# Two groups of row-tile products turned round and one transpose moved up, in the last stage of a four-block fused kernel

## The chip, the core and the metric

The kernel runs on one core of a Trainium2 chip. A core has five engines that run beside each other, each with its own queue of instructions: TensorE (PE, matrix products; its weight loads are shown apart as PEld), VectorE (DVE), ScalarE (ACT), GpSimd (POOL) and SyncE (SP), which here issues DMAs. Products are written to PSUM, in banks of 128 x 512 float32; the other operands lie in SBUF. The metric is the device time of one execution in microseconds (us).

## The reference, cut to what matters

The reference chains four blocks over `x` of 16 batches x 256 tokens x 256 features, each added to `x` through a gate: a resampler's cross attention, a top-2 mixture of experts, a masked cross attention, and at last a gated linear attention with a dense and a routed part. The change lies in the last one. Cut to what is touched:

```python
x = layernorm(x)
g1 = log_sigmoid(x @ Wg1a @ Wg1b + bg1) / 16     # decay of the dense part
g2 = log_sigmoid(x @ Wg2a @ Wg2b + bg2) / 16     # decay of the routed part
g  = x @ Wga @ Wgb                               # gate of the output
q1, k1, v = x @ Wq, x @ Wk, x @ Wv
...
o = chunked_attention(q1, k1, v, g1) + routed_attention(q2, k2, v, g2)
o = o * rsqrt(mean(o * o) + eps) * norm_w * (g * sigmoid(g))
out = x + tanh(gate) * (o @ Wo)
```

All products that share `x` and have narrow outputs (`Wqa`, `Wka`, `Wga`, `Wg1a`, `We`, `Wg2a`) are taken together, as one product with a matrix `la` of 256 columns; its result is called `low`.

## The kernel before, in words

Everything is float32, and a product shows in the profile as two records, its two passes. The last stage is the function `stage3_fast` (from L1619). It handles the 16 batches one after the other, and each batch in four slots, one for each pair of heads. A slot has a number `p` from 0 to 63; its batch is `p // 4`, and `p % 4` says which slot of the batch it is. The loop over `p` writes out the order of the work by hand: in each slot the main steps stand at fixed places, and small tables (`start`, `middle`, `rest`, `late`, `behind_mask`, `by_rows`, `logs`, L2036 to L2045) hang further steps on the slots. An entry `(f, d)` in list 0 to 3 calls `f` for batch `p // 4 + d` in that slot. Each engine runs its instructions in the order in which these calls issue them. Most instructions of VectorE, ScalarE and GpSimd show the line L50, that of a helper that records them, so they are told apart by the tiles that they write; products show L1637 and PE transposes L1640.

The main steps of a slot, in order: `masked(p - 1, 1)` (VectorE masks the second score block of the slot before, out of a PSUM tile of two banks called `sc`, of which there is one), `keys_queries(p + 1)` (products `kq`), the table `middle`, the table `rest`, `decays(p + 1)` (products `gq` and `gz`, then exponentials `ee` on ScalarE), the table `late`, `products(p, 0)` (products `sc<-f`), `masked(p, 0)` (VectorE, `at<-sc,amask`), the table `behind_mask`, `factors(p + 1)` (VectorE writes `f` from `kq` and `ee`, which frees the bank of `kq`), the table `by_rows`, `values` of the slot before (products `o`), `second(p + 1)` and `factors_second(p + 1)` (VectorE writes `q` from `gq` and `ee`, POOL writes `k`), the table `logs`, and `products(p, 1)` (products `sc<-q,k`). In the fourth slot `pairs` (products `both`, then VectorE's `em` and `am`) stands ahead of all.

Three steps matter here.

`turn_ahead(b)` (L1685) turns the normalised rows `xn` of the batch after next into `xnT`, with features on the partitions. VectorE transposes 32 x 32 squares in one instruction (`turned<-xn`), and 16 DMAs issued by SyncE (L1693) carry the squares to their places in `xnT`. There are two `xnT` buffers, for even and odd batches. It is called in the third slot, from the table `logs`, for batches 2 to 15. The first reader of the new `xnT` is `lows(b)` (L1695), two slots on, in the first slot of the next batch: eight passes `low<-xnT,la`, right behind `keys_queries`.

`lows(b)` also starts two DMAs that put copies of rows of `low` on other partitions: `lowd` (L1706, rows 0 to 63 copied to 64 to 127) and `low2` (L1708, rows 64 to 127 of the second 128 tokens copied to 0 to 63). With a copy on other partitions, two products with few rows lie in different row tiles of PE, which can run at the same time.

`all_gates(b)` (L1758), in the second slot, takes four products of 17 rows each: two that read `low` itself (row tiles from 64 and 96, tokens 0 to 127, written to two banks called `z`), and two that read `low2` (row tiles from 0 and 32, tokens 128 to 255, written to the tile `sc`). ScalarE reads the first `z` bank, then the two banks of `sc`; the second `z` bank is read later, by `gates_end`.

`outgates(b)` (L1811), in the first slot of its own batch, takes four products of 64 rows for the gate of the output: in turn one that reads `low` (rows 0 to 63) and one that reads `lowd` (rows 64 to 127), written to two banks called `zg`. The `lowd` that it reads was carried in the first slot of the batch before.

The order of each group, and the place of `turn_ahead`, as they stand before:

```python
                for i in range(2):
                    for n, (lo, hi) in enumerate(((0, 17), (32, 49))):
                        x, w = (low2[lo:hi, :], lbg2[lo:hi, :]) if i else (low[b][64 + lo:64 + hi, 1, tokens(0)],
                                                                         lbg[64 + lo:64 + hi, :])
                        matmul(two[:, n, :] if i else one[n], x, w, start=True, stop=True)
...
            behind_mask = {0: [(route_logits, 1)]}
...
                    2: [(gate_logs, 1, 1), (turn_ahead, 2), (normed_out, -1, 0), (normed_out, -1, 1)]}
```

Of the kernel before, what the change touches and what calls it, by code (L numbers as in the profile page):

```python
# [73 lines left out]
def layers(ctx: ExitStack, tc: tile.TileContext, t, out, check):  # L74
# [797 lines left out]
    def w3_load(name, shape, src=None):  # L872
        x = c3(name, shape)
        src = t[src or name]
        weights.append((x, src if len(src.shape) == len(shape) else src.rearrange("(k p) f -> p k f", p=P)))
        return x
# [3 lines left out]
    lbg = w3_load("lbg", [P, 512])  # L880
# [738 lines left out]
    def stage3_fast(early_bank):  # L1619

        with ExitStack() as sx:
# [3 lines left out]
            def of(b):  # L1625

                return w1 if b % 2 else w0

            def bank(name):
                return pss.tile([P, 512], F32, tag="ps", name=name) if pss else early_bank(name)  # L1630

            def tokens(i):
                return slice(i * P, (i + 1) * P)


            def matmul(*a, **k):
                tc.keep_in_program_order(nc.tensor.matmul(*a, **k))  # L1637
# [7 lines left out]
            lbg2 = w1.tile([P, 512], F32, tag="lbg2", name="lbg2")  # L1645
# [7 lines left out]
            xn, xnT, low, lg, hT, em, am, lowd = {}, {}, {}, {}, {}, {}, {}, {}  # L1653
# [104 lines left out]
            def all_gates(b):  # L1758

                lg[b] = of(b).tile([P, 2, 2, 512], F32, tag="lg", name="lg")  # L1760
                two = psa.tile([P, 2, 512], F32, tag="sc", name="sc")
                one = [bank("z"), bank("z")]
                for i in range(2):
                    for n, (lo, hi) in enumerate(((0, 17), (32, 49))):
                        x, w = (low2[lo:hi, :], lbg2[lo:hi, :]) if i else (low[b][64 + lo:64 + hi, 1, tokens(0)],
                                                                         lbg[64 + lo:64 + hi, :])
                        matmul(two[:, n, :] if i else one[n], x, w, start=True, stop=True)
                act3.activation(lg[b][:, 0, 0, :], one[0], AF.Exp, scale=-1.0)
                act3.activation(lg[b][:, 1], two, AF.Exp, scale=-1.0)
                z_[b, "z"] = one[1]  # L1770
# [40 lines left out]
            def outgates(b):  # L1811

                gw[b] = w2.tile([P, 4, S], F32, tag="gw", name="gw")
                two = [bank("zg"), bank("zg")]
                for i in range(2):
                    for h, (w, x) in enumerate(((lbg[0:64], low[b][0:64, 1, :]), (lbg2[64:], lowd[b][64:]))):
                        m = 2 * i + h
                        matmul(two[h][:, i * S:(i + 1) * S], w[:, m * P:(m + 1) * P], x, start=True, stop=True)
                for h, ps in enumerate(two):
                    e, zs = (w2.tile([P, 512], F32, tag=n, name=n) for n in ("eg", "zs"))  # L1820
                    act3.activation(e, ps, AF.Exp, scale=-1.0)
                    dve3.tensor_copy(zs, ps)
                    z_[b, h] = zs, e
# [205 lines left out]
            def warm():  # L2029

                ps = bank("warm")
                for _ in range(2):
                    matmul(ps, ones, v[B - 1][:, 0, :], start=True, stop=True)


            start = {3: [(pairs, 1)]}  # L2036
            middle = {0: [(lows, 1)], 1: [(all_gates, 1)], 2: [(turn_hot, 1)], 3: [(scaled_first, 0)]}

            rest = {0: [(bias, 2)], 2: [(turned_hot, 1), (norm_ahead, 2)], 3: [(steepest, 1, 0), (steepest, 1, 1)]}
            late = {1: [(norms, -1)], 2: [(vals, 1)], 3: [(project, -1)]}  # L2040
            behind_mask = {0: [(route_logits, 1)]}
            by_rows = {0: [(outgates, 0)], 1: [(gates_end, 1)]}
            logs = {0: [(route_sums, 1), (outgates_end, 0, 0)],
                    1: [(route, 1), (stats, 2), (outgates_end, 0, 1), (gate_logs, 1, 0)],
                    2: [(gate_logs, 1, 1), (turn_ahead, 2), (normed_out, -1, 0), (normed_out, -1, 1)]}  # L2045

            def run(steps, p):
                for f, d, *a in steps.get(p % 4, ()):
# [75 lines left out]
            b, p = B - 1, last - 1  # L2124
# [39 lines left out]
    if fast:  # L2164
        with tc.tile_pool(name="ctx_side", bufs=1) as keep, tc.tile_pool(name="f12w2", bufs=2) as keep2:
            prep = Prepare(keep, keep2, shared_bank)
            stage1_fast(keep, prep, shared_bank)
            s1.close()
            last_stage = stage3_fast(shared_bank)
            next(last_stage)  # L2170
            stage2_fast(prep, shared_bank, last_stage)
            next(last_stage)
        s_banks.close()
        for _ in last_stage:
            pass
    else:
        stage1()
        s1.close()
        stage2()
        s12.close()  # L2180
        stage3()
# [69 lines left out]
```

## Time and profile before

| What | Value |
|---|---|
| timed runs, median of three | 1838.59 us (1833.2 to 1842.05) |
| the profiled execution's own time | 1836.71 us |
| span of its records | 1834.8 us |
| mean granted TensorE clock | 0.995 |
| last stage's slots | from about 1237 to 1820 us |
| one batch of the last stage (start of its second slot's first `z` product to the next batch's) | 36.69 to 38.96 us |
| SyncE's issues of the 16 DMAs of one `turn_ahead` | 10.34 us for batch 8 |
| PE's wait for `xnT`, the longest one | 2.6 us |

The span is the time from the first record to the last; the execution's own time holds 1.9 us more around it. In the views, a row of the timeline has the start, the length, the engine, the line, the operation, the tiles written and read (`out<-in`), the form and the number of instructions that were merged into it; in brackets stands the idle time ahead of it and what ended that. In a view of waits a line has who waited, for whom, the total in us, how many times, and the longest. In the view of windows the columns are the stretch, its length, the busy time of each engine with the number of instructions, the granted TensorE clock as a share of full speed, and the DMA engines' share and rate.

### The profile page before, as it was taken

The page shows a single profiled execution, that of the slowest core. Times are in us where ns is not written, and L with a number is a line of the kernel's source. Part 1 is how long each engine was busy: PE and PEld are TensorE (multiplying, and loading weights), DVE is VectorE, ACT ScalarE, POOL GpSimd, SP SyncE. Part 2 cuts the span into 40 slices and gives each one's busy share as a digit, 9 for nine tenths or more (in the row PEclk, how much of TensorE's full clock was granted, in tenths as well). Part 3 has the DMA queues.
Part 4 walks back from the last instruction along what each step waited for, and adds up shares of the span by engine and source line. Part 5 has one row for each costly group of instructions (what it writes and reads, how often), then busy time and mean ns, then how long its engine had stood idle before and what let it go on. Part 6 is the DMA issues. An engine that isn't in the chain of part 4 may idle for free.

```text
span 1834.8 us, 35411 instructions
## 1 busy us (share of the span) xinstructions
PE 1802.7 (98%) x13930; PEld 1246.4 (68%) x13930; DVE 1138.6 (62%) x2695; ACT 832.4 (45%) x1727; POOL 1014.3 (55%) x1001
## 2 busy tenths in 40 slices
PE   8999999999999999999999999999999999999997
PEld 5666666666666666666777866656777777777775
DVE  3345656666656666666475388866666666666664
ACT  4433345343453334434343488744543454445432
POOL 3654766567666576656743766314454445444533
PEclk9999999999999999999999999999999999999999
DMA  9800010000010000000067933100111111111110
GB/s 298 235 1 22 16 35 13 28 17 20 27 35 10 29 20 10 28 24 17 13 221 246 251 56 48 21 3 11 38 28 36 29 37 28 34 31 32 33 31 26
DMA packets 110361, 98.05 MB, mean 53 GB/s; under 512 B 43835, under 2 KB 97763, under 8 KB 109673
## 3 DMA queue, kind: packets, MB, share of 16 engines
q1 hardware_dynamic: 97897, 78.91, 14.5%
q0 software_dynamic: 12288, 16.79, 4.5%
q8 instruction: 112, 1.84, 0.4%
q14 instruction: 64, 0.52, 0.1%
HBM read 52.03 MB, written 38.41 MB: 49 GB/s over the span
## 4 chain that ended last, share of the span: by engine, by line
PE 84%; POOL 7%; DVE 3%; issue 2%; ACT 2%; SPq 1%; DMA 1%; POOLq 0%; ACTq 0%; DVEq 0%
PE o L50 11%; PE qk L50 11%; PE v L50 9%; PE sc L50 8%; PE proj L50 7%; PE kq L1637 6%; PE sc L1637 6%; PE gq L1637 4%; POOL es L50 4%; PE ex L50 3%; PE v L1637 3%; PE o L1637 3%; PE proj L1637 2%; PE low L1637 2%; PE gz L1637 2%
## 5 line engine op out<-in xcount | busy, mean ns | idle before, releaser
L50 POOL TENSOR_SCALAR rs<-mv 128x2 f32<-128x2 f32 (+2 forms) x85 | 16.2, 190 | 404.4 <-DVE mv L50 402.6
L50 DVE RECIPROCAL rd<-o 128x256 f32<-128x256 f32 x64 | 112.3, 1754 | 155.0 <-PE o L50 155.0
L50 ACT ACTIVATE e<-sc 128x1024 f32<-128x1024 f32 (+1 forms) x192 | 181.5, 1015 | 18.5 <-PE sc L50 18.5
L50 POOL TENSOR_TENSOR at<-at,at 128x768 f32<-128x768 f32 x63 | 114.1, 1812 | 134.3 <-DVE at L50 134.3
L50 PE MATMUL sc<-qk 64*128 64x256 f32 (+1 forms) x1536 | 183.1, 384 | 0.5 <-DVE qk L50 0.5
L50 PE MATMUL o<-e,v 128*32 128x256 f32 (+1 forms) x3072 | 177.9, 379 | 0.0
L50 PEld LDWEIGHTS sc<-qk 64*128 64x128 f32 (+1 forms) x1536 | 132.0, 172 | 55.1 <-issue 26.8
L50 POOL TENSOR_TENSOR esum<-esum,es 128x512 f32<-128x512 f32 x128 | 163.2, 1275 | 10.0
L50 PE MATMUL qk<-kvT,wkv 128*128 128x333 f32 x512 | 164.3, 443 | 0.0
L50 POOL TENSOR_TENSOR es<-e 128x1024 f32<-128x1024 f32 x64 | 151.3, 2364 | 12.0 <-ACT e L50 9.0
L50 ACT ACTIVATE qk<-qk 128x256 f32<-128x256 f32 x128 | 48.7, 381 | 232.2 <-PE qk L50 232.2
L50 POOL TENSOR_TENSOR es<-es,e 77x1024 f32<-77x1024 f32 x64 | 150.3, 2349 | 5.0
L50 PEld LDWEIGHTS o<-e,v 128*32 128x32 f32 (+1 forms) x3072 | 99.8, 110 | 66.4
L50 DVE TENSOR_TENSOR at<-sc,amask 128x768 f32<-128x768 f32 x64 | 61.2, 957 | 133.7 <-PE sc L1637 78.2
L50 PE MATMUL qk<-kvT,wq 128*128 128x256 f32 x512 | 134.6, 385 | 0.0
L50 DVE COPY qk<-qk 128x333 f32<-128x333 f32 x128 | 64.6, 505 | 94.8 <-ACT qk L50 93.4
L50 POOL DMA_INDIRECT x<-rows_out,pos x64 | 100.9, 1577 | 35.6 <-issue 16.5
L50 PEld LDWEIGHTS qk<-kvT,wq 128*128 128x128 f32 x512 | 94.3, 189 | 35.1 <-issue 9.6
L50 PEld LDWEIGHTS qk<-kvT,wkv 128*128 128x128 f32 x512 | 97.2, 190 | 30.0
L50 PE MATMUL proj<-wo0h,oT 128*128 128x256 f32 x512 | 113.7, 380 | 0.3 <-DVE oT L50 0.3
L50 PE MATMUL v<-wkv,kvT 128*128 128x512 f32 x256 | 113.1, 595 | 0.0
L50 PEld LDWEIGHTS proj<-wo0h,oT 128*128 128x128 f32 x512 | 96.0, 190 | 13.9 <-issue 0.8
(267 smaller groups left out, 3920.8 us busy)
## 6 DMA issues: line engine op xcount, KB each, us to landing
rows<-zero SPq DMA_DIRECT2D x16, 640.0 KB
xin<-rows SPq DMA_DIRECT2D x16, 640.0 KB
r<-rms SPq DMA_DIRECT2D x30, 256.0 KB
rows_out<-y SPq DMA_DIRECT2D x16, 384.0 KB
v<-vctx SPq DMA_DIRECT2D x15, 308.0 KB
x<-in_x_dram SPq DMA_DIRECT2D x16, 256.0 KB
rows_out<-y SPq DMA_DIRECT2D x16, 256.0 KB
out_dram<-x SPq DMA_DIRECT2D x15, 256.0 KB
```

Source lines behind the costliest of these rows:

```text
L50: x = getattr(self.engine, name)(*a, **k)
L1637: tc.keep_in_program_order(nc.tensor.matmul(*a, **k))
```

## The change

Three edits. In `all_gates` the two products that read `low2` now stand ahead of the two that read `low`. In `outgates` each pair now begins with the product that reads `lowd`; which bank each product writes stays as it was. And `turn_ahead` moves from the table `logs` to the table `behind_mask`, still in the third slot: its transpose now stands on VectorE right behind `masked(p, 0)` and ahead of `f` and `q` of the next slot. The 16 DMAs keep their place in SyncE's order, and the instructions of ScalarE and POOL keep theirs. No instruction is added or removed but for semaphore waits.

```diff
@@ all_gates
-                for i in range(2):
+                for i in (1, 0):
                     for n, (lo, hi) in enumerate(((0, 17), (32, 49))):
@@ outgates
                 for i in range(2):
-                    for h, (w, x) in enumerate(((lbg[0:64], low[b][0:64, 1, :]), (lbg2[64:], lowd[b][64:]))):
+                    for h, w, x in ((1, lbg2[64:], lowd[b][64:]), (0, lbg[0:64], low[b][0:64, 1, :])):
                         m = 2 * i + h
@@ tables of stage3_fast
-            behind_mask = {0: [(route_logits, 1)]}
+            behind_mask = {0: [(route_logits, 1)], 2: [(turn_ahead, 2)]}
...
-                    2: [(gate_logs, 1, 1), (turn_ahead, 2), (normed_out, -1, 0), (normed_out, -1, 1)]}
+                    2: [(gate_logs, 1, 1), (normed_out, -1, 0), (normed_out, -1, 1)]}
```

## The prediction

> **What bounds the kernel now.** I read the page first: busy times, then the chain that ended last.
>
> ```profile
> PE 1802.7 (98%) x13930; PEld 1246.4 (68%) x13930; DVE 1138.6 (62%) x2695; ACT 832.4 (45%) x1727; POOL 1014.3 (55%) x1001
> ...
> PE 84%; POOL 7%; DVE 3%; issue 2%; ACT 2%; SPq 1%; DMA 1%; POOLq 0%; ACTq 0%; DVEq 0%
> ```
>
> TensorE (PE) is busy nearly all the time and owns 84% of the chain. So an edit pays only where it takes a wait of PE away, and costs only where it adds one. The change lies in the last stage, from about 1237 to 1820 us. The view of waits over that stretch, for PE alone, has one large entry:
>
> ```profile
> PE low L1637 <- DMA xnT<-turned: 3.7, 4, 2.6
> ```
>
> These are the products of `lows`, the first readers of the rows that `turn_ahead` carries by 16 DMAs. The view counts only gaps over 150 ns, so I went to the timeline of PE. `lows` stands behind the four query passes of `keys_queries`, and follows them at once when its rows are there:
>
> ```profile
> 1267.82 1.03 PE L1637 MATMUL kq<-xnT,wq 128*128 128x256 f32 x4
> 1271.46 3.60 PE L1637 MATMUL low<-xnT,la 128*128 128x256 f32 x8 [2.61 <-DMA xnT<-turned]
> ...
> 1604.44 1.03 PE L1637 MATMUL kq<-xnT,wq 128*128 128x256 f32 x4
> 1605.31 1.89 PE L1637 MATMUL low<-xnT,la 128*128 128x256 f32 x8
> ...
> 1752.31 1.03 PE L1637 MATMUL kq<-xnT,wq 128*128 128x256 f32 x4
> 1753.74 1.99 PE L1637 MATMUL low<-xnT,la 128*128 128x256 f32 x8 [0.40 <-DMA xnT<-turned]
> ```
>
> The pair at 1604 is clean: `low` starts 0.87 us behind the start of the query row. At 1752 it is 1.43, so 0.56 us is lost; at 1267 it is 3.64, so 2.77 us is lost. The same subtraction for batches 3 to 15 gives 0, 0.38, 0.23, 0, 0.30, 0.05, 0.34, 0.01, 0, 0.04, 0.60, 0.22, 0.56: 2.7 us.
>
> The change by its two halves follows.
>
> **The transpose, moved up.** The timelines of DVE and SP around one `turn_ahead` (batch 8):
>
> ```profile
> 1480.26 0.96 DVE L50 TENSOR_TENSOR at<-sc,amask 128x768 f32<-128x768 f32 x1 [3.79 <-POOL k L50]
> 1481.13 0.68 DVE L50 TENSOR_TENSOR f<-kq,ee 128x512 f32<-128x512 f32 x1
> 1481.73 0.41 DVE L50 TENSOR_TENSOR q<-gq,ee 128x256 f32<-128x256 f32 x1
> 1482.07 0.71 DVE L50 STREAM_TRANSPOSE turned<-xn 128x512 f32<-128x512 f32 x1
> 1483.11 0.42 DVE L50 SCALAR_TENSOR_TENSOR em<-both,dmask 128x256 f32<-128x256 f32 x1 [0.32 <-PE both L1637]
> ...
> 1482.85 10.34 SPq L1693 DMA_DIRECT2D xnT<-turned  x16
> ```
>
> SP's 16 issues start 0.07 us behind the transpose's end and take 10.34 us. The rows land some 1.3 to 1.8 us later (`low` starts that far behind the last issue wherever it waited). From the transpose's start that is 12.4 to 13.1 us, while PE reaches `lows` 12.54 us after it (1482.07 to 1494.61). The two are even, which is why some batches wait and others don't.
>
> Now the transpose goes behind `at`, ahead of `f` and `q`: it starts at 1481.13, 0.94 us earlier. Its input `xn` was ready (ScalarE's two rows ended at 1477.65). SP's queue keeps its order and is empty there (the row before, `r<-rms`, ended at 1474.40), so all 16 DMAs move up by 0.94. That is more than every loss in batches 3 to 15 (at most 0.60), so those waits go. The `low` row also shortens from about 1.97 to 1.89, since the first weight load no longer waits. As a cross-check I took the start of the first `z` product in each batch's second slot: the periods are 38.96, then 36.72 to 37.38, the shortest 36.69 with no wait in it. From 1281.82 to 1762.49 there are 13 periods, 480.67 us; 13 x 36.69 is 476.97. Gain **3.70 us**, the row shortening included.
>
> What is delayed: `f` and `q` by one transpose, 0.62 us as DVE starts its next (0.71 less the overlap that the rows show). `f` then ends at 1482.43; it frees the bank that PE's next `kq` product takes at 1483.00, so 0.5 us of cover. `q` ends at 1482.77, ahead of `em`, which waits for PE until 1483.11 anyway. So DVE is level again before anyone asks: cost 0. If that cover were gone it would be at most 0.62 x 14 = 8.7 us.
>
> Batch 2 keeps a wait, because its first slots have no `proj` products to fill the time: its gap goes from 2.61 to 1.67 us, gain **0.94**. There is more in that batch. Its `low` row lasts 3.60 us and not 1.97, and the windows view says why:
>
> ```profile
> 1271.40:1275.20 3.80, 3.74 (x11) 3.12 (x12) 0.10 (x1) 0.00 (x0) 0.00 (x0) 0.56 0.02 4
> ```
>
> The granted clock, third from the end, is 0.56 behind the gap; 3.60 - 1.97 = 1.63 us is the price. Whether a 1.67 us gap still brings it, this trace can't say outright. Stretches of 3.41 us in which PE was busy for 0.90 us (1267.94 to 1271.36) and 2.74 us (1223.57 to 1226.98) were followed by half clock; stretches with 2.25 (from 1052.91) and 2.51 (from 1206.50) weren't. The new stretch would have 1.74 or more, depending on where the gap falls. The bounds are 0 and 1.63; I take **1.63**, the nearest row being 2.25, but not by much. [...]
>
> **The products, turned round.** `all_gates` (15 times) and `outgates` (16 times). Batch 7's `all_gates` on PE, DVE and ACT:
>
> ```profile
> 1466.57 0.70 PE L1637 MATMUL z<-lbg,low 17*128 17x512 f32 x2
> 1467.09 0.70 PE L1637 MATMUL sc<-lbg,low 17*128 17x512 f32 x2
> 1467.10 0.59 PE L1637 MATMUL z<-lbg,low 17*128 17x512 f32 x2
> ...
> 1468.15 0.71 PE L1637 MATMUL gq<-dmask,lg 128*128 128x128 f32 x4
> ...
> 1469.80 0.81 PE L1637 MATMUL sc<-f 64*128 64x256 f32 x6
> ...
> 1465.66 1.37 DVE L50 SCALAR_TENSOR_TENSOR at<-sc,kden,am 128x256 f32<-128x256 f32 x4
> ...
> 1467.72 0.60 ACT L50 ACTIVATE lg<-z 128x512 f32<-128x512 f32 x1 [1.47 <-PE z L1637]
> 1468.26 1.02 ACT L50 ACTIVATE lg<-sc 128x1024 f32<-128x1024 f32 x1
> ```
>
> The `sc` pair is the one with the DMA's rows, but its DMA was issued 5 us before and no view shows a wait for it. What holds `sc` is its PSUM bank, which DVE's masking frees at 1467.03. `z`, in other row tiles, runs in that time, and its second pass runs beside `sc`'s first. With `sc` first, PE waits until 1467.09 with both pairs; then all four run side by side. `sc` ended the group before and ends it after (`z` is some 0.013 us behind it): +0.013 x 15 = **0.2 us**. No gain is possible here, since `sc` starts no earlier.
>
> But ACT gets `z` later. Its order is `z` first, then `sc`, and it waits for `z` already. `z`'s second pass moves from 1467.10 to 1467.64, so `lg<-z` starts at 1468.26, `lg<-sc` at 1468.80, and that ends at 1469.82 where it ended at 1469.29. PE's `sc<-f` takes the bank that `lg<-sc` frees, 0.055 us after it: 1469.87, and not 1469.80. The first group shows this wait in pure form: `lg<-sc` at 1245.09 for 1.02 us and `sc<-f` at 1246.17. So +0.075 x 14 = **1.05 us**; in the first group, whose masking ends 0.54 us later still, **0.54**. ACT's next rows slide by 0.54 us and have room: it is idle for 0.47 us at 1472.2 and 1.8 at 1474.7.
>
> `outgates` alternates between the lower 64 rows (`low`) and the upper 64 (`lowd`); its DMA is a whole batch old. The group ends with the upper tile in both orders, which is busy with `sc<-f` until 1461.60 in both. ACT reads it only at 1463.2. Cost 0, bounded by one start's shift of 0.13 x 16 = 2.1 us.
>
> **Sum.** -3.70 - 0.94 - 1.63 + 0.2 + 1.05 + 0.54 = -4.5 us. The profiled execution took 1836.71 us (span 1834.8 and 1.9 around it), so 1832.2 for one like it. The median of the three timed runs, 1838.59, lies 1.88 above it: **1834.1 us**.
>
> **Rivals.** (a) Half clock stays in batch 2: 1834.1 + 1.63 = 1835.7. For it, the stretch with 2.74 us busy; against it, the two with 2.25 and 2.51. (b) The moved transpose starts no DMA earlier, the change not doing what it says: the waits view of SP names `PE both` for 11 of these issues. Then the products' price alone is left, 1838.59 + 1.8 = 1840.4. Against it: SP issued at 1482.85 while `both` ran until 1483.07. (c) Slower: the four products of `all_gates` don't run side by side after the DVE wait, and `z` comes a pass behind `sc`: 0.53 x 15 = 8.0, so 1842.1. It decides from 0.3 us per group on (4.5 / 15). Against it: `sc` at 1467.09 and `z` at 1467.10 ran together. (d) Row tiles start strictly in program order, so the lower tile in `outgates` waits for the upper one: up to 2.1, 1836.2. Against it: `sc<-f` starts at 1460.72, ahead of the second `sc<-ident` (1460.83) which stands before it. [...]
>
> **How the numbers follow.** Forecast 0.46, (a) 0.33, (b) 0.08, (c) 0.05, (d) 0.05, others 0.03. The three runs span 1833.2 to 1842.05, so a median carries some 3 us of its own: 1829.5 to 1840.5, which takes in (a), (b) and (d). Over 0.5% (9.2 us, about what a measurement of this kernel can tell from no change) needs twice my gain, or more than (c): faster 0.05, same 0.91, slower 0.04.
>
> **What would show it.** Right: `turned` directly behind `at`, SP's issues 0.94 us earlier, no `low` wait after batch 2, periods near 36.75; `sc` and `z` of `all_gates` starting together near 0.8 us behind the last query pass; `sc<-f` just behind `lg<-sc`. Wrong: `low` still waiting (b), `kq` of the fourth slot waiting for `f`, or `gq` more than 0.1 us later behind `sc` (c). A batch period above 37 would refute the sum.

## The result, and the profile after

The changed kernel takes a median of 1832.13 us (1829.14 to 1833.99, seven runs). The kernel before, on the same chip, takes 1838.59 us (1833.2 to 1842.05, seven runs). The ratio is 0.9967, with a 95% interval of 0.9951 to 0.9982: 6.1 us less, by the interval 3.3 to 9.0. The forecast was 1834.1. The profiled execution took 1833.27 us, span 1831.5, mean granted clock 0.997.

The page of after, its first row and its shares of the chain, answers to the first fence of the prediction:

```profile
PE 1793.7 (98%) x13930; PEld 1242.3 (68%) x13930; DVE 1137.3 (62%) x2695; ACT 832.2 (45%) x1727; POOL 1015.0 (55%) x1001
...
PE 81%; DVE 7%; POOL 7%; ACT 2%; issue 2%; DMA 1%; SPq 0%; POOLq 0%; DVEq 0%; ACTq 0%
```

PE still bounds the kernel, with the same number of instructions. New is VectorE's 7% of the chain where it had 3%; that share comes with the turned `all_gates` (e2 and e7 have it too, e1 has 3%). The view of PE's waits in the last stage shows what changed places, in three lines of after and then one of before:

```profile
PE sc L1637 <- DVE at L50: 8.8, 17, 1.1
PE low L1637 <- DMA xnT<-turned: 1.7, 1, 1.7
...
PE sc L1637 <- ACT lg L50: 0.6, 1, 0.6
```

```profile
PE sc L1637 <- DVE at L50: 1.4, 2, 1.1
```

Waits for the turned rows fell from four (3.7 us) to one (1.7). Waits of `sc` for the masking rose from two (1.4 us) to 17 (8.8). That entry is not a loss of that size: most of it is the 0.46 us of each batch in which `z` used to run, and which now stand ahead of four products that run side by side. The last line of after is new, the first group's wait for ScalarE. What the two do cost is worked out below.

The timelines of VectorE and SyncE around the `turn_ahead` of batch 8 in the changed kernel:

```profile
1478.39 0.96 DVE L50 TENSOR_TENSOR at<-sc,amask 128x768 f32<-128x768 f32 x1 [3.78 <-POOL k L50]
1479.26 0.70 DVE L50 STREAM_TRANSPOSE turned<-xn 128x512 f32<-128x512 f32 x1
1479.89 0.65 DVE L50 TENSOR_TENSOR f<-kq,ee 128x512 f32<-128x512 f32 x1
1480.46 0.41 DVE L50 TENSOR_TENSOR q<-gq,ee 128x256 f32<-128x256 f32 x1
1481.24 0.42 DVE L50 SCALAR_TENSOR_TENSOR em<-both,dmask 128x256 f32<-128x256 f32 x1 [0.37 <-PE both L1637]
```

```profile
1480.03 10.34 SPq L1693 DMA_DIRECT2D xnT<-turned  x16
```

The transpose stands 0.87 us behind the start of `at`, where it stood 1.81 us behind (1482.07 - 1480.26): 0.94 us earlier. SyncE begins 0.07 us behind its end, as before, and takes the same 10.34 us. VectorE still has 0.37 us to spare ahead of `em`.

On PE the first readers of those rows are clean in batch 8, and batch 2 keeps one wait:

```profile
1491.88 1.03 PE L1637 MATMUL kq<-xnT,wq 128*128 128x256 f32 x4
1492.74 1.89 PE L1637 MATMUL low<-xnT,la 128*128 128x256 f32 x8
...
1269.42 1.03 PE L1637 MATMUL kq<-xnT,wq 128*128 128x256 f32 x4
1272.12 1.97 PE L1637 MATMUL low<-xnT,la 128*128 128x256 f32 x8 [1.68 <-DMA xnT<-turned]
```

That wait is 1.68 us where it was 2.61, and the row behind it takes 1.97 us and not 3.60: the granted clock is 1.00 there, by the windows view.

```profile
1272.00:1274.50 2.50, 2.38 (x14) 2.20 (x15) 0.38 (x2) 0.00 (x0) 0.74 (x1) 1.00 0.03 7
```

`all_gates` of batch 7 on PE, and ScalarE's two readers:

```profile
1463.67 1.03 PE L1637 MATMUL kq<-xnT,wq 128*128 128x256 f32 x4
1465.15 0.70 PE L1637 MATMUL sc<-lbg,low 17*128 17x512 f32 x2 [0.46 <-DVE at L50]
1465.17 0.70 PE L1637 MATMUL z<-lbg,low 17*128 17x512 f32 x2
1465.69 0.59 PE L1637 MATMUL sc<-lbg,low 17*128 17x512 f32 x2
1465.70 0.59 PE L1637 MATMUL z<-lbg,low 17*128 17x512 f32 x2
...
1467.93 0.92 PE L1637 MATMUL sc<-f 64*128 64x256 f32 x8
```

```profile
1466.37 0.60 ACT L50 ACTIVATE lg<-z 128x512 f32<-128x512 f32 x1 [2.05 <-PE z L1637]
1466.87 1.02 ACT L50 ACTIVATE lg<-sc 128x1024 f32<-128x1024 f32 x1
```

All four products run in pairs, 0.015 us apart. `lg<-sc` ends at 1467.89 and `sc<-f` follows at 1467.93.

**Where the time went.** As a measure I took the stretch from the last query pass ahead of the first `all_gates` group to the one ahead of the 15th, 14 batch periods. It was 519.63 us (1242.55 to 1762.18) and is 515.04 (1243.61 to 1758.65): **4.59 us less**. The first period went from 38.96 to 36.92, the others from between 36.69 and 37.38 down to between 36.75 and 36.91. The two spans differ by 3.3 us only, because the changed kernel's profile came 1.06 us late to the last stage, in work that the change doesn't touch, and lost 0.23 behind it. The timed difference, 6.1, holds 4.6 well inside its interval.

### The profile page after: what moved, and what is told of

Read it like the earlier page. It is cut to its first block, busy times and chain, and to the rows that moved or that the text cites. A ratio compares the mean times of both kernels' runs of the same rounds, so it can differ in the third digit from the quotient of the medians.

```text
span 1831.5 us, 35425 instructions
## 1 busy us (share of the span) xinstructions
PE 1793.7 (98%) x13930; PEld 1242.3 (68%) x13930; DVE 1137.3 (62%) x2695; ACT 832.2 (45%) x1727; POOL 1015.0 (55%) x1001
## 3 DMA queue, kind: packets, MB, share of 16 engines
q8 instruction: 112, 1.84, 0.4%
## 4 chain that ended last, share of the span: by engine, by line
PE 81%; DVE 7%; POOL 7%; ACT 2%; issue 2%; DMA 1%; SPq 0%; POOLq 0%; DVEq 0%; ACTq 0%
PE o L50 12%; PE qk L50 11%; PE v L50 9%; PE sc L50 8%; PE proj L50 7%; PE sc L1637 5%; PE kq L1637 5%; POOL es L50 4%; PE gq L1637 3%; PE v L1637 3%; PE proj L1637 3%; PE ex L50 3%; DVE at L50 2%; PE o L1637 2%; POOL rs L50 2%
```

## The experiments

Eight kernels were run. Each was timed against the kernel before on its own chip; e1 to e4 shared one, e5 to e8 another. Theory: the moved transpose is the whole gain, and the turned products are a small loss through ScalarE. Rivals: the products' order matters (either way), and the clock behind batch 2's gap is what paid.

### e1: the transpose alone

```diff
-            behind_mask = {0: [(route_logits, 1)]}
+            behind_mask = {0: [(route_logits, 1)], 2: [(turn_ahead, 2)]}
...
-                    2: [(gate_logs, 1, 1), (turn_ahead, 2), (normed_out, -1, 0), (normed_out, -1, 1)]}
+                    2: [(gate_logs, 1, 1), (normed_out, -1, 0), (normed_out, -1, 1)]}
```

> The transpose moved up alone, both groups of products in their old order. Theory A (the gain is the transfer's wait, the products' order costs): the whole gain and none of the cost, so 1.8 us below the changed kernel and 6.3 us below the kernel before; batch periods of the last stage fall to 36.69 us, the products that read the new rows start 0.87 us behind the start of the query row in batches 3 to 15, batch 2 keeps a gap of about 1.67 us with the granted clock at full speed. Theory B (the products' order is what gained): no faster than before by more than 0.1%, periods still 36.7 to 37.4.

Measured: 1829.19 us (1827.73 to 1833.26, seven runs) against 1835.61 (24 runs of before): ratio 0.9964, 0.9949 to 0.9978. By time this can't be told from the whole change. By the trace it can: the 14 periods take 513.40 us, **1.64 less** than with the products turned, and those from the second on are 36.69 where the changed kernel has 36.76 in most. Some 0.25 of the 1.64 us is probably not the products' doing: batches 13 to 15 of the changed kernel's execution have periods of 36.85, 36.91 and 36.78, where SyncE's 16 issues took 11.06 to 11.35 us (10.34 in batch 8). That leaves about 1.4 us for the products. PE's longest waits of e1 in the last stage:

```profile
PE low L1637 <- DMA xnT<-turned: 1.7, 1, 1.7
PE sc L1637 <- DVE at L50: 1.4, 2, 1.1
```

The one wait of batch 2 is that of the changed kernel (1.68), and `sc` waits as little as before. So the move makes all of the gain, and the turned products give some of it back.

### e2: only the order in all_gates

```diff
-                for i in range(2):
+                for i in (1, 0):
```

> Only the order of the four products of all_gates is changed. Theory A: 1.8 us slower than the kernel before (0.1%, at the edge of what can be timed); in the trace PE idles until the masking on VectorE frees the bank, the four products then start together 0.83 us behind the last query pass (1.38 in the first group), sc<-f comes at 3.62 and not at 3.55 us behind it, and the wait for the 16 DMAs stays as in the kernel before (single waits up to 0.6 us, 2.6 us and half clock in batch 2). Theory B: 4 us or more faster.

Measured: 1837.01 us (12 runs), ratio 1.0003, 0.9993 to 1.0014. PE's waits in the last stage:

```profile
PE sc L1637 <- DVE at L50: 8.8, 17, 1.1
PE low L1637 <- DMA xnT<-turned: 3.0, 3, 2.6
```

Both entries are there: the order alone brings the 17 waits for the masking, and does not take away those for the rows. A period without such a wait is 36.76, as in the changed kernel, against 36.69 in e1. The cost is some 0.07 us a batch, and the timing, +0.6 us with an interval of -1.3 to +2.6, has room for it and not for a gain of several us.

One thing came out otherwise than expected. Batch 2 waited as long as before, 2.64 us, but kept the full clock:

```profile
1273.00:1275.00 2.00, 1.98 (x10) 1.79 (x11) 0.00 (x0) 0.00 (x0) 0.00 (x0) 1.00 0.03 8
```

So this run parts the move from the clock. Its 14 periods take 518.71 us and those of the changed kernel 515.04, and neither has half clock in them: the move gains 3.7 us with no help from the clock (`outgates`, in which the two also differ, is worth nothing by e3).

### e3: only the order in outgates

```diff
-                    for h, (w, x) in enumerate(((lbg[0:64], low[b][0:64, 1, :]), (lbg2[64:], lowd[b][64:]))):
+                    for h, w, x in ((1, lbg2[64:], lowd[b][64:]), (0, lbg[0:64], low[b][0:64, 1, :])):
```

> Only the order of the pairs of outgates is changed. Theory A: no difference, the group takes as long from its first product to the first o<-at,v behind it, the two row tiles still overlap. Strict order of starts (rival d): up to 0.13 us more per group, 2.1 us in all, and the product of the lower tile starts behind that of the upper one. Theory B: part of the gain, over 1 us.

Measured: 1834.94 us (10 runs), ratio 0.9999, 0.9987 to 1.0011. The group in PE's timeline of e3:

```profile
1462.52 0.39 PE L1637 MATMUL zg<-low,lbg 64*128 64x256 f32 x1
1462.53 0.27 PE L1637 MATMUL sc<-f 64*128 64x128 f32 x1
1462.64 0.38 PE L1637 MATMUL zg<-lowd,lbg 64*128 64x256 f32 x1
...
1463.29 0.38 PE L1637 MATMUL zg<-lowd,lbg 64*128 64x256 f32 x1
```

In e3's program `zg<-lowd` stands first. In the trace `zg<-low` still starts first, 0.12 us ahead. It starts 0.01 us ahead of the last `sc<-f`, which lies in the upper rows as `zg<-lowd` does, and `zg<-lowd` 0.11 us behind that one's start; before, with the other order in the program, the distances were the same (1461.48, 1461.49 and 1461.60). The products `o` behind the group start 1.83 us after the slot's first row of `sc` products (1461.76 to 1463.59), where before it was 1.84. The edit moves nothing. Rival (d) is refuted.

Here the wait of batch 2 was 2.66 us, and the clock fell to 0.55 behind it (1272.40 to 1276.20 in the windows view).

### e4: the transpose moved, and batch 2's rows prepared one slot earlier

On top of e1, for the first batch's slots only; the tables then skip the three steps where they stood:

```diff
+            early = {("rest", 1): [(stats, 2)], ("mask", 1): [(norm_ahead, 2)], ("logs", 1): [(turn_ahead, 2)]}
```

> The transpose moved up as in the change, products in their old order, and for batch 2 alone the moments, the normed rows and the transpose stand one slot earlier, so that its 16 DMAs start when the last reader of the buffer is done. Theory A: batch 2's gap of 1.67 us goes as well, so 1.7 us below the kernel with the transpose alone moved, 3.4 below the changed kernel and 8 below the kernel before; what could take it back is VectorE or ScalarE in the second slot of the first batch, by up to 1 us. If the gap of batch 2 stays, what holds those rows is not the time of the transfer.

Measured: 1830.04 us (six runs), ratio 0.9961, 0.9946 to 0.9975. The wait for the rows is gone, yet the first period fell from 36.40 us in e1 to 35.62 only, by 0.78 of the 1.67 us that were expected. Part of what is late next shows in the timeline of e4:

```profile
1251.27 1.27 POOL L50 TENSOR_TENSOR gw<-zs,eg 128x512 f32<-128x512 f32 x1 [2.44 <-ACT eg L50]
1251.29 1.27 DVE L50 TENSOR_TENSOR eq<-eq,ec 128x8 f32<-128x8 f32 x1
...
1252.60 0.17 DVE L50 TENSOR_TENSOR hot<-eq,e 128x8 f32<-128x8 f32 x1
...
1252.82 0.38 PE L1640 MATMUL hT<-ident,hot 128*4 128x128 f32 x2 [0.97 <-DVE hot L50]
```

PE waits for `hot`, the routing of the next batch. The transpose stood ahead of the routing on VectorE and made it 0.63 us late (1249.71 to 1250.34). One of its operations (`eq<-eq,ec`) then fell on POOL's `gw`, and with eight columns took as long as POOL's did, 1.27 us.

### e5: the same, with the transpose behind the routing

The three early steps run behind the tables' own steps and not ahead of them, so that VectorE's order is `hot` and then the transpose.

> As the kernel with batch 2's steps one slot earlier, but its transpose stands on VectorE behind the routing of the next batch and not ahead of it, so that the one-hot rows, for which PE waited 0.97 us there, are not late. Theory A: batch 2's gap of 1.67 us goes and nothing comes back, so 1.7 us below the kernel with the transpose alone moved, about 8 us (0.44%) below the kernel before; the first batch period is about 34.7 us where that kernel has 36.4. If 36 us or more stay, another wait takes the place of the gap.

Measured: **1827.65 us** (1826.27 to 1829.94, six runs) against 1835.79 (23 runs of before): ratio 0.9954, 0.9938 to 0.9969, 8.4 us less than before. The first period is 34.49, against 36.40 in e1. Batch 2 in PE's timeline:

```profile
1267.30 1.03 PE L1637 MATMUL kq<-xnT,wq 128*128 128x256 f32 x4
1268.17 1.89 PE L1637 MATMUL low<-xnT,la 128*128 128x256 f32 x8
```

0.87 us from one row's start to the other's: nothing is lost. A loss of 0.17 us is left in batch 13. By the median this is the fastest of all kernels here, with the old order of the products; its interval overlaps that of e1, so that the gain over e1, a first period that is 1.91 us shorter, rests on the trace.

### e6: four more transposes in the way of f

On top of e1, `turn_ahead` computes something extra: four small transposes into a tile that nobody reads.

```diff
+                spare = w1.tile([P, P], F32, tag="spare", name="spare")
+                for n in range(4):
+                    dve3.transpose(spare, xn[b].rearrange("p k (i d) -> p (k i) d", i=2)[:, n, :])
```

> The transpose moved up alone, and behind it four more transposes of 128x128 into a spare tile that nobody reads, so that f and q on VectorE come about 0.9 us later (estimated between the rows of 128x64, 0.24 us, and 128x512, 0.71 us). Theory A (the transpose's 0.62 us was hidden by a cover of some 0.5 us at the bank of kq): the cover is used up, kq of the fourth slot waits for f by about 0.4 us in each of 14 batches, 5.7 us above the kernel with the transpose alone moved, near the kernel before. If f's delay is hidden by more than I think, no change; if every VectorE instruction in that place counts fully, 0.9 x 14 = 12.6 us.

Measured: 1837.82 us (10 runs), ratio 1.0015, 1.0005 to 1.0025. VectorE in e6, and PE's waits:

```profile
1478.89 1.31 DVE L50 STREAM_TRANSPOSE spare<-xn 128x128 f32<-128x128 f32 x4
1480.12 0.65 DVE L50 TENSOR_TENSOR f<-kq,ee 128x512 f32<-128x512 f32 x1
```

```profile
PE kq L1637 <- DVE f L50: 8.8, 14, 0.6
```

The four delay `f` by 1.23 us (1478.89 to 1480.12); I had taken 0.9, and so expected too little. A period grew from 36.69 to 37.39, by 0.70. Only the first hardly grew (36.40 to 36.46), since there the delay falls into batch 2's wait for its rows. The 14 periods take 522.87 us, 9.5 more than in e1; by the two ratios e6 is 9.4 above e1. So 0.53 us of the further delay was covered and the rest was paid in full. In e1 `f` ends at 1476.28 and the `kq` that takes its bank starts at 1476.87, which gives the same 0.53 when about 0.06 us is allowed for the release, an estimate from `sc<-f`, which followed `lg<-sc` by 0.055 us before. The cover that the prediction put at 0.5 us is real.

### e7: ScalarE reads sc first

On top of the whole change, to test the path through ScalarE:

```diff
-                act3.activation(lg[b][:, 0, 0, :], one[0], AF.Exp, scale=-1.0)
                 act3.activation(lg[b][:, 1], two, AF.Exp, scale=-1.0)
+                act3.activation(lg[b][:, 0, 0, :], one[0], AF.Exp, scale=-1.0)
```

> The changed kernel, with ScalarE reading the two banks of sc first and the bank of z behind them. Theory A (the order's price is the late reading, through the banks that it frees): sc<-f no longer waits for lg<-sc, but the products ms, which stand ahead of it and take the first z bank, wait until lg<-z ends: ms moves from 2.99 to about 3.6 us behind the last query pass and pushes sc<-f from 3.61 to about 4.2, 0.6 us more in 14 batches, 8 us above the changed kernel, while the first group, which has no ms, gets about 0.5 us back. If the price was the row tiles' order, nothing changes.

Measured: 1838.72 us (10 runs), ratio 1.0015, 1.0003 to 1.0026, some 8.8 us above the changed kernel by the two ratios. ScalarE and PE in e7, batch 7:

```profile
1465.25 1.02 ACT L50 ACTIVATE lg<-sc 128x1024 f32<-128x1024 f32 x1 [2.01 <-PE z L1637]
1466.17 0.59 ACT L50 ACTIVATE lg<-z 128x512 f32<-128x512 f32 x1
```

```profile
1466.81 0.64 PE L1637 MATMUL ms<-sq,halves 128*32 128x256 f32 x8 [0.51 <-ACT lg L50]
1467.38 0.81 PE L1637 MATMUL sc<-f 64*128 64x256 f32 x6
```

`lg<-z` frees its bank later (at 1466.76), and PE's `ms` takes it 0.05 us after that. Each period is 0.53 us longer (37.29 against 36.76). Only the first batch gains, where `sc<-f` comes 0.53 us earlier. 14 x 0.53 - 0.53 is 6.9 us; the rest of the 8.8 lies within the two intervals. So PE is paced here by the order in which ScalarE empties these three banks, and reading `z` first is the better one.

### e8: the transpose later

Before, with `turn_ahead` behind `em` and `am` in the fourth slot:

```diff
-            start = {3: [(pairs, 1)]}
+            start = {3: [(pairs, 1), (turn_ahead, 2)]}
```

> The kernel before with the transpose moved the other way, into the fourth slot behind em and am, about 1.85 us later. Theory A (transfer and work are level, every delay of the transpose beyond that is a wait of PE): each of 14 batches waits 1.85 us longer, 26 us in all, and PE's gaps of about 2 us bring half clock in some of the batches, 1.6 us each, so 26 to 48 us slower than before (1.4% to 2.6%). If the rows are not what low waits for, or the DMAs don't start with the transpose, under 5 us.

Measured: 1863.24 us (four runs), ratio 1.0145, 1.0125 to 1.0165, 27 us more than before. PE's waits:

```profile
PE low L1637 <- DMA xnT<-turned: 26.3, 14, 3.9
```

Every batch waits, 1.9 us on average: the DMAs follow the transpose in both directions. Of the 14 waits, four were followed by half clock (0.50 to 0.66 in the stretches behind them) and ten were not. The stretches behind two of them, both of 1.90 us, in the windows view:

```profile
1389.00:1390.90 1.90, 1.90 (x10) 1.69 (x11) 0.00 (x0) 0.00 (x0) 0.36 (x1) 1.00 0.12 40
...
1701.80:1704.60 2.80, 2.80 (x9) 2.28 (x10) 0.00 (x0) 0.00 (x0) 0.37 (x1) 0.66 0.09 30
```

The gap was the same; the clock behind it was 1.00 once and 0.66 once.

## Why the prediction was right, step by step

The sum was -4.5 us and the last stage's stretch gives -4.59. So close a match has some luck in it, since two smaller misses cancel below. The forecast on the median, 1834.1, lies 2.0 us above the measured 1832.13, where the seven runs of either kernel spread over 4.9 and 8.9 us. Part by part the trace can be read with e1 between the two: the move was priced at 3.70 + 0.94 + 1.63 = 6.27 us and brought 6.23 (519.63 - 513.40); the products were priced at 1.79 and cost about 1.4, and some 0.25 us of waits stayed that were forecast as gone.

- **The move.** The transpose 0.94 us earlier, the DMAs with it, 1.68 us of wait (forecast 1.67) in batch 2: right. Of the losses in batches 3 to 15, forecast as gone, 0.08 and 0.15 us are left, in batches 13 and 14, where SyncE's issues took longer (e1). Rival (b), DMAs that start no earlier, falls by SyncE's row, and e8 shows the same dependence in the other direction.
- **The cover.** 0.5 us was claimed, 0.53 measured (e6).
- **The products.** The size was `sc<-f` 0.075 us later per batch, 0.54 in the first, `gq` 0.013 later. Measured: `sc<-f` 3.61 to 3.62 us behind the last query pass (3.55 before), 4.16 in the first group (3.62 before), `gq` 1.071 us behind `sc` (1.058). e7 shows that the path is the one named, ScalarE and the banks that it frees. Rival (c) falls: the four products ran in pairs, 0.015 us apart.
- **outgates.** 0, as forecast (e3).
- **The clock.** -1.63 us was right for the profiled pair: half clock behind the gap of 2.61 (0.56 over 3.80 us), full clock behind 1.68 (1.00). The working went by PE's busy time in a stretch of 3.41 us, and put the new stretch at 1.74 us or more. That is what the changed kernel has, with full clock behind it:

```profile
1269.29:1272.70 3.41, 1.74 (x9) 1.24 (x8) 0.80 (x4) 0.00 (x0) 3.16 (x3) 1.00 0.10 17
```

So rival (a) did not happen. But the choice rested on a row far off, 2.25 us, and there luck helped: in e8, half clock still followed 1.56 us, only 0.18 us less. By the gap's length alone nothing could be said: full clock followed 2.64 us (e2) and half clock 1.85 us (e8). So the term comes in some executions only: with the transpose unmoved, before (0.56) and e3 (0.55) had half clock there and e2 (1.00) hadn't; with gaps of 1.68 to 1.86 us, after, e1 and e7 had none.

Without the clock the working stands at -4.64 + 1.79 = -2.9 us; up to 1.63 more comes or doesn't by the execution. The timed interval, 3.3 to 9.0 us less, holds the sum with the clock, and just misses the one without.

## What to carry to other kernels

Here a transfer started 0.94 us earlier when the instruction that ends last ahead of it, a transpose on VectorE, was moved up by as much, and the price is read where the instructions that it passes free a bank: `f` came 0.63 us later and still had 0.53 us to spare. Putting the products with the latest-looking operand first gained nothing where that operand's DMA was issued 5 us before; here such a group waits for its output bank (0.46 us in batch 7), and what it then costs is set by the order in which the next engine empties the banks (0.07 us a batch with `z` read first, 0.53 more with `sc` first, e7). And a stage's first batch, which lacks the filling work of the others, is worth an order of its own (e5: 1.9 us more in one period).

## What the runs showed of the hardware that was not expected

**Half clock is not a matter of the gap's length alone.** In e8, gaps of 1.85, 1.90, 2.04 and 3.88 us were followed by half clock, another of 1.90 and nine from 1.50 to 1.70 were not; e2's gap of 2.64 us wasn't either. In the execution of before, the granted clock fell to 0.50 and rose again at 1226.98, 1233.81, 1271.36 and 1274.77 us: 6.83, 37.55 and 3.41 us apart, 2, 11 and 1 times 3.41. Steps of 3.41 us from such a change divide an execution into stretches, also where the clock stays full. Three of them that hold a gap, two of e8 and then one of e2:

```profile
1385.24:1388.65 3.41, 1.83 (x8) 1.27 (x8) 1.47 (x6) 0.00 (x0) 2.50 (x3) 1.00 0.21 43
1463.74:1467.16 3.41, 1.56 (x8) 1.05 (x7) 0.40 (x3) 0.00 (x0) 3.05 (x3) 1.00 0.35 96
```

```profile
1268.80:1272.21 3.41, 1.57 (x8) 1.04 (x6) 1.22 (x6) 0.00 (x0) 2.75 (x3) 1.00 0.15 24
```

Only the second was followed by half clock. Its gap of 1.85 us lay inside the stretch; the first holds a part of a gap of 1.90 us, and the third of the 2.64 us. So in the last stage half clock followed such stretches with PE busy for 0.90 us (before) and 1.56 (e8), and not those with 1.57 (e2), 1.74 (after) and 1.83 (e8). Ahead of the last stage that order does not hold: stretches with 2.74 us (before) and 2.87 (after) were followed by half clock, while those with 2.25 and 2.51 (before) weren't. Why that is so is open.

**A second stretch of half clock can move an execution by some 3 us.** It lies ahead of the last stage, in code that no kernel here changes. The windows view of the same stretch, of before and then of e1 (after's clock there is 0.69 too, and that of e2, e3 and e4):

```profile
1226.00:1237.00 11.00, 10.53 (x45) 7.33 (x45) 5.65 (x11) 2.99 (x9) 2.57 (x5) 0.69 0.01 1
```

```profile
1226.00:1237.00 11.00, 10.51 (x73) 8.32 (x73) 7.34 (x15) 4.54 (x13) 4.04 (x7) 1.00 0.03 7
```

With 0.69, about half clock for 6.8 us, the first group's last query pass stands at 1242.55 to 1243.61 (before, after); with 1.00 at 1239.51 to 1240.27 (e1, e6, e7, e8). So some 3 us of a difference between two spans can say nothing of the kernel, and a difference of a few us has to be read inside the stage.

**A small VectorE operation can take as long as POOL's beside it.** The view of e4's tile `eq` gives the shortest, median and longest of 15 in ns:

```profile
L50 DVE TENSOR_TENSOR eq<-eq,ec x15: 166/168/1272, 1251.3 to 1763.5; 128x8 f32<-128x8 f32 x15
```

The one of 1272 ns is the one that lies on `gw` of POOL (1251.29 against 1251.27, both 1.27 us long); in e1 all 15 take 166 to 169. This is one case, and what made the two take equally long was not tested.

**Products in different row tiles can start out of the program's order.** `zg<-low` started 0.12 us ahead of `zg<-lowd`, which stands before it in the program (e3). So PE did not start all its products in the order in which the calls issue them.
